# Statistics of the first layer on VectorE for six batches in place of three, under a rewritten order of steps, in a two-layer graph kernel

## The chip, the cores and the metric

The kernel runs on one core of a Trainium2 chip. The metric is the device time of one execution in microseconds (us). The kernel before was run three times: 2301.16, 2302.13 and 2302.11 us, median 2302.11.

The core's engines run side by side, each through its own queue of instructions in order: PE (TensorE) multiplies matrices, DVE (VectorE), ACT (ScalarE) and POOL (GpSimd) work on tiles, SP (SyncE) issues most of the DMA transfers, ACT and POOL issue some. An instruction starts when those ahead of it on its engine are through and the semaphores that it waits for have been raised.

## The reference, cut to what matters

`x` is 32 batches of 512 channels by 1024 nodes, in float32. Two residual layers follow one another:

```python
# layer 0: attention over nodes, mixed by adj
h = relu(layernorm(x))                       # over the 1024 nodes
q, k = wq . h, wk . h                        # one number per node
s = leaky_relu(q[n] + k[m], 0.01)
att = softmax(s, over n)
x = x + relu(adj @ (h @ att^T) + bm)
# layer 1: two graph products
h = relu(layernorm(x))
x = x + ((support * kernel) applied to h) + bias     # support and kernel are both adj
```

The layer norm divides by the root of the variance plus 1e-5. Both layers need the mean and the variance of every row of 1024 elements: 4 tiles of 128 channels per batch and layer.

## The kernel before, in words

**The work of a batch.** The score of a pair is a sum of two numbers under a leaky ReLU. So the softmax is not taken over a 1024 by 1024 matrix: nodes are sorted by q, and for each m the sums over the nodes above and below a threshold come out of running totals. A batch goes through these steps, each a function in the kernel:

- `load` (L309, SP) brings four tiles of 128x1024. `stats` (L315 on) takes mean and variance of one tile. `norm` and `slopes` turn them into a scale and a shift, `relu` (L366, ACT) applies them.
- `scores` (L375, PE) gives q and k, which go through DRAM and come back as a row on all partitions (`row`). `rank` (L417 to L426, DVE) counts, for 128 nodes, how many q are smaller; `lower` (L433, ACT) counts against k. `value` (L474, PE) is adj times h for 128 nodes, `spread` (L481, ACT) copies it from PSUM, and `scatter` (L487, POOL) writes it by rank to a DRAM table `td`.
- `fetch` (L503, SP) reads the sorted rows into the tiles `vs`. `weights` (L512 and after, ACT) takes the exponentials, `later`, `totals` (L535, L536, PE) and `stationary` (L546, POOL) prepare the running sums.
- `scan` (L562, and L559 for the middle one, PE) makes the running sums of 128 rows with a triangular matrix; nine scans (0 to 8) per batch, each from both ends. The last row of one scan must be in the next one's input: `sums` (L574 copies the result out of PSUM on ACT) carries that row over. For batches 5 to 27 (`LO = 5`, `HI = 4`) it is carried by two DMAs of 2 KB on SP (L576, L577, `vs<-t` in the profile); for the others by two copies on ACT (L572, L573). Two more DMAs (L580, L581) put the sums into `td`.
- `gather` (L586, POOL) fetches the rows for each m, into one buffer `G` that all batches share. `excess`, `divide`, `weigh` (L611, ACT) and `combine` (L615, DVE) make the softmax's result, `turn` (L622 PE, L626 DVE) transposes it, adds it to x and leaves row sums for layer 1.
- Layer 1: `means`, `stats` (the Square alone, L337), `norm`, `slopes`, `relu`, then the graph product: `seed`, `mix`, `propagate` (L657, PE) and `finish` (L670, L674, DVE) in a form with seven half-size products; the last four batches (`PLAIN = 4`) use plain products (`plain`, L689). `store` (L701, SP) writes the result.

**Statistics of layer 0.** `stats` has two ways. For `s.b < DIRECT` it runs on DVE: two `bn_stats` of 128x512 (L324) and one `bn_aggr` (L325) per tile. For other batches it runs on ACT: one `Identity` (L334) and one `Square` (L337) of 128x1024 per tile, each with an accumulated sum.

**The order.** All steps of all batches, 5935 of them, are issued in one fixed order that stands in the string `ORDER`: two characters in base 36 per step, which name the kind of step and how many steps of that kind to skip ahead. `tc.manual_schedule()` keeps that order on every engine's queue. So the steps of four to six batches are interleaved: while batch 14 scans, batch 12 is in its second layer, 13 is gathered, 16 is ranked and 17 loaded. In the steady part the order repeats every 187 steps, one batch. Bounded buffers add waits: 8 PSUM banks, 16 tiles for x and h (`xp`), 5 fetched tiles (`vsp`), 2 tiles for sums (`tp`) and one `G`.

The switch and the scan's carry, as they stand before:

```python
if layer == 0 and s.b < DIRECT:          # DIRECT = 3
    ...
    nc.vector.bn_stats(st[:, i, :], s.x[c][:, ts(i, HALF)])
    nc.vector.bn_aggr(s.mv[:, c, :], st.rearrange("p i s -> p (i s)"))
    return
...
nc.scalar.copy(t[:, 0:C], p)             # sums, of scan i
if i < NB - 1 and LO <= s.b < B - HI:
    nc.sync.dma_start(s.vs[ha - 1][0:1, 0:C], t[0:1, 0:C])
    nc.sync.dma_start(s.vs[hb + 1][HP : HP + 1, 0:C], t[HP : HP + 1, 0:C])
```

Of the kernel before, what the change touches and what calls it, by code (L numbers as in the profile page):

```python
# [26 lines left out]
DIRECT = 3  # L27
# [6 lines left out]
0a0405002u2y2w302u2y01022w30342y362w352u3730342w322u332y3538303b3639033a2i102j2k180u0d090v12080n0l  # L34
0q0g0x130s370p0f320o0z150b0m0i0t0y33170r0h380c3b110e1639343a1i0w190j061d0k10352w302y1j142z2i361e2l
0u1f371g2m321b2j2k180v1a33121h380x1c133b0z0l0n150q2l0y0g0s2n170p0f39110o0i160m0h0w190t3a070e0r101i
1d2o312u0j2w142u1b0u2p0k1a1c2m2q2i3u3v1j1k1e2k180v1t1f2j1g121l131h0x1u1m150z0n0l3w1v2l1n0g0q0y1w0f
0s1o170i0p111x0h0o1p0e160m0w2n1y1i1a0j191b341q2y0k2x1d2v1z1j1e351r1f141g0t1h0r362m1c3732332o382p2q
3u3b1k20391s3a1t2i3v1l2k21101u2j1m18220u1v3w25291n120l0n270v1w262l280g0q1o23130x1x240f0s0i1p0p0z15
0h2n1y0o0e1q170m0y1i1d1z0j1b340k1a1r11161j1e352r1f362s0w1g191h0t141c0r2e2m375e2d5d322c332a5c385b2o  # L40
59553b2p56202q3u5a1k391s3a1t2i3v1l2k21102f2g5g1u5i5h5f0u2j2b18582h575k5j1m123m3q1v3w3n3t3r3o0n1n3p
0q3s0v221w250s0l290p1o270x2t130g1x26283e2l231p0f0z3h242n1y0i3g1q150h3f0y1z0e3c0o3d1r1i1d17113j0j3i
1b0m4t1a4u3l0w0k3k4w16344v1j1e41302x2r3x422s1f352y4g1g434n3y3z444f191h4036454m2z464i2o0t2p474x3u20
4y4p49500r4z4k1s141c4h37482m513v212q1k324r2e4b332d2c5e385c4a2u4j1t5b594d4o3b5a1l5d392w4l524c3a531u
2i4q1m314e2a2v3w1v55562k104s2j2f2g542b5i2h585k1n18570u5j1w5h5g0l0n1o0q5f3m3n1x3o3p3q3t0s1p123r0p3s
2n0v221y250g291q13272t0x0f3e261z282l231r0i3h240z153g0h3f0y0e173c0o3d0m1i1a113j0j3i1b340k1d0w4t3l1j
1g3k4u4w351f41304v312z2x424g3x2r202s434n3y1s4f3z4044161e2136454m464i191h0t472o4x4y0r4z49502e4p372p
484h3u5e3v2d5d4b324r2c332a4a5c2f384j554d3b2y4o5652395b4c593a5a2q2g2u1k4q2b2i5i2w582v574e5h5g1t5f2k
104s2h4k2j5k545j514l1l2m1853141c3m3n1u3o3p3q3t1m0n3r3s1v3w0u220q250s290l1n12270p0v2t261w0g283e2l23
1o0x240f1x3h0i1p133g0z0h2n1y0e3f1q153c1i1d0o0y3d1z0j1b3j1a1r0k3i110m4t3l4u1j1g3k4w0w342r4v3x2s3y43  # L50
2z3z313530444f171f454m2y1640201e414i2o1s4g191h2p42363u2q3v46144n0t1c2e1k4x0r4p474y1t4z3750485e5d4k
2149324r2d332c1l4h2a5c38514b553b565b4a394j2u593a4d5a2w4o1u2f2m4c2g2b2h2i2v4q2x58525k4e5i572k104s5j
542j5h5g5f1m4l18533m3n1v3w3o3p3q3t3r3s0n0u220q250s291n0l12270p0v261w2t0g3e283f232l0x240f3g131o3h0i
0z1x3c0o3d150h3j0y3i0e0m4t3l4u1p3k1i1d114w342n4v1b0j1y1a3x2r410k3y35444g1j1g3z434m172s401f1645194f
361e424i1h2e464n0t5e2d5d0w0r4x4y2c4p2a502f4z2g554830141c5c312b2z562o1q2y582h4r492p1z5k3u375b2q1k4h
4a5i5932574b332u4o385j524c3b4j5a395h1r2x4q3a4d5g2w5f202m1t4e2i4s4l102v54532j1s181l213v2k3m1u3n3o3p
3q3t3r3s0u220n250q290s1m0l2747120p3w2t0g1v260v3e284k3h0f23513g0x242l0i3f1n133c0z0o0h1w0m3d150e3j0y
3i1i1d340j1b1o4t113l1a4u0k1x3k354w414v1j1g422r4g3x2s3y1p171f4n3z43162n1y1e4044194f1h36454m2h0t465k
5j2b4i0r0w4x4y2g4p2f502a4z2c55482d305831141c5c2e2z49562o2y4r5b1q4h2p4a375i3u59574b2u4o1z5e322q1k4j
4c335a52385h4d3b2w4q2x5d395g1r2v5f3a4e4l2m201t2i4s1054532j1s181l213v2k3m1u3n3o3p3q3t3r3s0u220n250q  # L60
291m0l0s270v121v3w2t0p0g263e282l0x230f3h24131n3g0i47151w3f0h0z3c0o3d0m4k0e511o3j0y1x1i1d3i0j341b11
4t1a4u3l0k3k354w1p4v411j1g2n1y2r3x422s171f3y4g3z444n40161e1943364m1h454f2e0t5e465d2d4i0r5c0w4x2c4y
2a4p2f502g4z2b485530141c31562o2z5b2h1q2v4r492p581z3u5i372q1k4h4a5k5932574b332x4o385j524c3b4j5a395h
1r2y4q3a4d5g2u5f202m1t4e2i4s4l102w54532j1s181l213v2k3m1u3n3o3p3q3t3r3s0u220n250q290s1m0l2747120p3w
2t0g1v260v3e284k3h0f23513g0x242l0i3f1n133c0z0o0h1w0m3d150e3j0y3i1i1d340j1b1o4t113l1a4u0k1x3k354w41
4v1j1g422r4g3x2s3y1p171f4n3z44162n1y1e4043194m1h36454f2e0t465e5d2d4i0r0w4x4y2c4p2a502f4z2g55482b30
5c31141c562h2z495b2o2v4r581q4h2p4a375i3u5k592q2x1k4o1z4b5732335j384c4j523b5a5h4d2y394q2u5g3a1r5f2w
4l4e2m53201t2i4s10541s181l2j213v2k3m1u3n3o3p3q3t3r3s0u220n250q290s1m0l2747120p3w2t0g1v260v3e284k3h
0f23513g0x242l0i3f1n133c0z0o0h1w0m3d150e3j0y3i1i1d340j1b1o4t113l1a4u0k1x3k354w414v1j1g422r4g3x2s3y
1p171f4n3z44162n1y1e4043194m1h36454f2e0t465e5d2d4i0r0w4x4y2c4p2a502f4z2g55482b305c31141c562h2z495b  # L70
2o2v4r581q4h2p4a375i3u5k592q2x1k4o1z4b5732335j384c4j523b5a5h4d2y394q2u5g3a1r5f2w4l4e2m53201t2i4s10
541s181l2j213v2k3m1u3n3o3p3q3t3r3s0u220n250q290s1m0l2747120p3w2t0g1v260v3e284k3h0f23513g0x242l0i3f
1n133c0z0o0h1w0m3d150e3j0y3i1i1d340j1b1o4t113l1a4u0k1x3k354w414v1j1g422r4g3x2s3y1p171f4n3z44162n1y
1e4043194m1h36454f2e0t465e5d2d4i0r0w4x4y2c4p2a502f4z2g55482b305c31141c562h2z495b2o2v4r581q4h2p4a37
5i3u5k592q2x1k4o1z4b5732335j384c4j523b5a5h4d2y394q2u5g3a1r5f2w4l4e2m53201t2i4s10541s181l2j213v2k3m
1u3n3o3p3q3t3r3s0u220n250q290s1m0l2747120p3w2t0g1v260v3e284k3h0f23513g0x242l0i3f1n133c0z0o0h1w0m3d
150e3j0y3i1i1d340j1b1o4t113l1a4u0k1x3k354w414v1j1g422r4g3x2s3y1p171f4n3z44162n1y1e4043194m1h36454f
2e0t465e5d2d4i0r0w4x4y2c4p2a502f4z2g55482b305c31141c562h2z495b2o2v4r581q4h2p4a375i3u5k592q2x1k4o1z
4b5732335j384c4j523b5a5h4d2y394q2u5g3a1r5f2w4l4e2m53201t2i4s10541s181l2j213v2k3m1u3n3o3p3q3t3r3s0u
220n250q290s1m0l2747120p3w2t0g1v260v3e284k3h0f23513g0x242l0i3f1n133c0z0o0h1w0m3d150e3j0y3i1i1d340j  # L80
1b1o4t113l1a4u0k1x3k354w414v1j1g422r4g3x2s3y1p171f4n3z44162n1y1e4043194m1h36454f2e0t465e5d2d4i0r0w
4x4y2c4p2a502f4z2g55482b305c31141c562h2z495b2o2v4r581q4h2p4a375i3u5k592q2x1k4o1z4b5732335j384c4j52
3b5a5h4d2y394q2u5g3a1r5f2w4l4e2m53201t2i4s10541s181l2j213v2k3m1u3n3o3p3q3t3r3s0u220n250q290s1m0l27
47120p3w2t0g1v260v3e284k3h0f23513g0x242l0i3f1n133c0z0o0h1w0m3d150e3j0y3i1i1d340j1b1o4t113l1a4u0k1x
3k354w414v1j1g422r4g3x2s3y1p171f4n3z44162n1y1e4043194m1h36454f2e0t465e5d2d4i0r0w4x4y2c4p2a502f4z2g
55482b305c31141c562h2z495b2o2v4r581q4h2p4a375i3u5k592q2x1k4o1z4b5732335j384c4j523b5a5h4d2y394q2u5g
3a1r5f2w4l4e2m53201t2i4s10541s181l2j213v2k3m1u3n3o3p3q3t3r3s0u220n250q290s1m0l2747120p3w2t0g1v260v
3e284k3h0f23513g0x242l0i3f1n133c0z0o0h1w0m3d150e3j0y3i1i1d340j1b1o4t113l1a4u0k1x3k354w414v1j1g422r
4g3x2s3y1p171f4n3z44162n1y1e4043194m1h36454f2e0t465e5d2d4i0r0w4x4y2c4p2a502f4z2g55482b305c31141c56
2h2z495b2o2v4r581q4h2p4a375i3u5k592q2x1k4o1z4b5732335j384c4j523b5a5h4d2y394q2u5g3a1r5f2w4l4e2m5320  # L90
1t2i4s10541s181l2j213v2k3m1u3n3o3p3q3t3r3s0u220n250q290s1m0l2747120p3w2t0g1v260v3e284k3h0f23513g0x
242l0i3f1n133c0z0o0h1w0m3d150e3j0y3i1i1d340j1b1o4t113l1a4u0k1x3k354w414v1j1g422r4g3x2s3y1p171f4n3z
44162n1y1e4043194m1h36454f2e0t465e5d2d4i0r0w4x4y2c4p2a502f4z2g55482b305c31141c562h2z495b2o2v4r581q
4h2p4a375i3u5k592q2x1k4o1z4b5732335j384c4j523b5a5h4d2y394q2u5g3a1r5f2w4l4e2m53201t2i4s10541s181l2j
213v2k3m1u3n3o3p3q3t3r3s0u220n250q290s1m0l2747120p3w2t0g1v260v3e284k3h0f23513g0x242l0i3f1n133c0z0o
0h1w0m3d150e3j0y3i1i1d340j1b1o4t113l1a4u0k1x3k354w414v1j1g422r4g3x2s3y1p171f4n3z44162n1y1e4043194m
1h36454f2e0t465e5d2d4i0r0w4x4y2c4p2a502f4z2g55482b305c31141c562h2z495b2o2v4r581q4h2p4a375i3u5k592q
2x1k4o1z4b5732335j384c4j523b5a5h4d2y394q2u5g3a1r5f2w4l4e2m53201t2i4s10541s181l2j213v2k3m1u3n3o3p3q
3t3r3s0u220n250q290s1m0l2747120p3w2t0g1v260v3e284k3h0f23513g0x242l0i3f1n133c0z0o0h1w0m3d150e3j0y3i
1i1d340j1b1o4t113l1a4u0k1x3k354w414v1j1g422r4g3x2s3y1p171f4n3z44162n1y1e4043194m1h36454f2e0t465e5d  # L100
2d4i0r0w4x4y2c4p2a502f4z2g55482b305c31141c562h2z495b2o2v4r581q4h2p4a375i3u5k592q2x1k4o1z4b5732335j
384c4j523b5a5h4d2y394q2u5g3a1r5f2w4l4e2m53201t2i4s10541s181l2j213v2k3m1u3n3o3p3q3t3r3s0u220n250q29
0s1m0l2747120p3w2t0g1v260v3e284k3h0f23513g0x242l0i3f1n133c0z0o0h1w0m3d150e3j0y3i1i1d340j1b1o4t113l
# [690 lines left out]
```

## Time and profile before

| | before |
|---|---|
| median of three runs | 2302.11 us |
| profiled execution | 2301.56 us |
| its span | 2299.8 us |
| PE busy | 2215.1 us (96%) |
| DVE busy | 1719.3 us (75%) |
| ACT busy | 1730.8 us (75%) |
| POOL busy | 716.9 us (31%) |
| mean granted clock of PE | 0.988 |
| DMA | 657.77 MB, 286 GB/s on the mean |

All times in the profile are of one execution on the chip and count from the start of its span. The span is a little shorter than the execution's time; the 1.8 us around it are the same kind of overhead in every run. A table by stretch gives each engine's busy time between two moments. A wait is written as the engine and line that waited, an arrow, and what it waited for, with the total, the count and the longest. The chain of work that ended last is followed back from the last instruction: at each step to what released it, or to the instruction before it on its engine; it is listed as start, length, engine, tile and line. `x8` behind an instruction is a count.

### The profile page before, as it was taken

The page shows a single profiled execution, that of the slowest core. Times are in us where ns is not written, and L with a number is a line of the kernel's source. Part 1 is how long each engine was busy: PE and PEld are TensorE (multiplying, and loading weights), DVE is VectorE, ACT ScalarE, POOL GpSimd, SP SyncE. Part 2 cuts the span into 40 slices and gives each one's busy share as a digit, 9 for nine tenths or more (in the row PEclk, how much of TensorE's full clock was granted, in tenths as well). Part 3 has the DMA queues.
Part 4 walks back from the last instruction along what each step waited for, and adds up shares of the span by engine and source line. Part 5 has one row for each costly group of instructions (what it writes and reads, how often), then busy time and mean ns, then how long its engine had stood idle before and what let it go on. Part 6 is the DMA issues. An engine that isn't in the chain of part 4 may idle for free.

```text
span 2299.8 us, 28792 instructions
## 1 busy us (share of the span) xinstructions
PE 2215.1 (96%) x7344; PEld 946.6 (41%) x7344; DVE 1719.3 (75%) x4840; ACT 1730.8 (75%) x3317; POOL 716.9 (31%) x979
## 2 busy tenths in 40 slices
PE   6978999999999999999999999999999999999897
PEld 3423443444444444444444444344444444443343
DVE  6746777878778778877877877877877787777453
ACT  4699889776778777777877777877777887787752
POOL 2343223333323333233333222333332333224210
PEclk9989999999999999999999999999999999999999
DMA  6676878888889888888888878888888888877961
GB/s 225 234 282 232 282 293 309 313 298 295 274 291 324 296 311 291 286 291 317 308 310 298 298 267 310 317 301 305 294 275 290 323 300 305 311 246 277 356 243 64
DMA packets 217717, 657.77 MB, mean 286 GB/s; under 512 B 39376, under 2 KB 39504, under 8 KB 217552
## 3 DMA queue, kind: packets, MB, share of 16 engines
q1 hardware_dynamic: 153760, 362.16, 46.7%
q0 software_dynamic: 57344, 276.86, 31.3%
q10 hardware_dynamic: 6448, 16.92, 2.8%
q8 instruction: 59, 0.97, 0.2%
q14 instruction: 106, 0.87, 0.1%
HBM read 438.05 MB, written 217.01 MB: 285 GB/s over the span
## 4 chain that ended last, share of the span: by engine, by line
PE 77%; DMA 8%; ACT 6%; DVE 5%; issue 2%; POOL 1%; SPq 0%; ACTq 0%; POOLq 0%; DVEq 0%
PE pv L474 34%; PE pg L657 26%; PE sc L562 9%; PE tr L622 3%; DMA td<-t 3%; PE pq L375 2%; DVE g L615 2%; DMA g<-td,idg 2%; PE pp L689 1%; PE sc L559 1%; ACT junk L433 1%; DVE y L626 1%; ACT junk L337 1%; DMA td<-v,idx 1%; DMA vs<-t 1%
## 5 line engine op out<-in xcount | busy, mean ns | idle before, releaser
L474 PE MATMUL pv<-wmT,x 128*128 128x512 f32 x2048 | 917.5, 596 | 0.0
L474 PEld LDWEIGHTS pv<-wmT,x 128*128 128x128 f32 x2048 | 380.5, 190 | 489.1 <-issue 452.1
L487 POOL DMA_INDIRECT td<-v,idx x256 | 270.7, 1057 | 659.5 <-issue 283.5
L657 PE MATMUL pg<-h,wsq 128*128 128x512 f32 x896 | 412.4, 602 | 2.5 <-DVE y L674 2.0
L615 DVE SCALAR_TENSOR_TENSOR g<-g,cf 128x512 f32<-128x512 f32 x512 | 375.2, 764 | 17.2 <-ACT g L611 14.0
L586 POOL DMA_INDIRECT g<-td,idg x256 | 244.8, 956 | 299.2 <-DVE y L626 95.2
L433 ACT ACTIVATE junk<-qrow,qk 128x1024 uint8<-128x1024 f32 x256 | 292.8, 1144 | 30.3 <-DMA qrow<-qd 19.9
L562 PE MATMUL sc<-vs,sm 128*64 128x512 f32 x1024 | 284.0, 621 | 7.8 <-ACT vs L572 5.8
L657 PEld LDWEIGHTS pg<-h,wsq 128*128 128x128 f32 x896 | 163.3, 190 | 243.3 <-issue 180.9
L574 ACT COPY t<-sc 128x512 f32<-128x512 f32 x288 | 167.6, 582 | 99.2 <-PE sc L562 41.6
L481 ACT COPY v<-pv 128x512 f32<-128x512 f32 x256 | 147.4, 578 | 124.3 <-PE pv L474 77.4
L546 POOL TENSOR_TENSOR sm<-mask_a,wc 128x192 f32<-128x192 f32 x96 | 63.2, 658 | 521.4 <-PE sc L562 455.9
L657 PE MATMUL pg<-mx,wmix 128*128 128x512 f32 x448 | 209.4, 599 | 0.0
L366 ACT ACTIVATE x<-x,nmr,rstd 128x1024 f32<-128x1024 f32 x128 | 149.3, 1230 | 78.2 <-DVE nmr L359 78.2
L670 DVE SCALAR_TENSOR_TENSOR y<-pg,bm_sb,y 128x512 f32<-128x512 f32 x224 | 166.4, 745 | 45.9 <-PE pg L657 45.5
L422 DVE TENSOR_SCALAR_CACHE_REDUCE junk<-qrow,qk,cnt 128x128 uint8<-128x128 f32 (+6 forms) x224 | 180.4, 805 | 8.2
L626 DVE SCALAR_TENSOR_TENSOR y<-tr,nbm,y 128x512 f32<-128x512 f32 x256 | 174.7, 746 | 15.3 <-PE tr L622 12.4
L417 DVE TENSOR_SCALAR_CACHE_REDUCE junk<-qrow,qk 128x896 uint8<-128x896 f32 (+6 forms) x224 | 165.7, 740 | 18.6 <-DMA qrow<-qd 16.7
L674 DVE TENSOR_TENSOR y<-pg,y 128x512 f32<-128x512 f32 x168 | 115.1, 685 | 81.6 <-PE pg L657 81.1
L611 ACT ACTIVATE g<-g,cf 128x512 f32<-128x512 f32 x256 | 168.6, 709 | 3.4 <-DVE cf L605 1.7
L337 ACT ACTIVATE junk<-y,nm 128x1024 uint8<-128x1024 f32 x128 | 146.7, 1146 | 31.4 <-DVE nm L345 29.6
L366 ACT ACTIVATE h<-y,nmr,rstd 128x1024 f32<-128x1024 f32 x128 | 154.0, 1235 | 2.6 <-DVE nmr L359 2.6
(135 smaller groups left out, 2496.4 us busy)
## 6 DMA issues: line engine op xcount, KB each, us to landing
vs<-td SPq DMA_DIRECT2D x96, 792.0 KB
td<-t SPq DMA_DIRECT2D x576, 132.0 KB
x<-in_x_dram SPq DMA_DIRECT2D x128, 512.0 KB
y<-in_x_dram SPq DMA_DIRECT2D x128, 512.0 KB
out_dram<-y SPq DMA_DIRECT2D x128, 512.0 KB
qrow<-qd ACTq DMA_DIRECT2D x32, 512.0 KB
vs<-t SPq DMA_DIRECT2D x368, 2.0 KB
td<-v,idx POOLq DMA_INDIRECT x256, 6.3
```

Of the source, the lines that this page charges most:

```text
L337: nc.scalar.activation(junk, s.x[c], AF.Square, bias=s.nm[:, c : c + 1], scale=1.0 / ROOT, accum_out=s.var[:, c : c + 1],)
L366: nc.scalar.activation(h, s.x[c], AF.Relu, bias=s.nmr[:, c : c + 1], scale=s.rstd[:, c : c + 1])
L422: nc.vector.tensor_scalar(junk[:, j * P :], s.qrow[:, j * P :], qc, first, ALU.is_lt, ALU.add, accum_out=s.cnt[:, 1, j : j + 1],)
L433: nc.scalar.activation(junk, s.qrow, AF.Sign, bias=s.qk[:, 1, j : j + 1], accum_out=s.sgn[:, j : j + 1])
L474: nc.tensor.matmul(pv, s.h[c][:, ts(j, P)], wmT[:, c, :], start=(c == 0), stop=(c == NC - 1))
L487: i = nc.gpsimd.indirect_dma_start(tds[s.b % TABLES][:, :], bass.IndirectOffsetOnAxis(ap=s.idx[j // 4][:, j % 4 : j % 4 + 1], axis=0), v[: ...
L562: nc.tensor.matmul(p[ts(k, HP), :], m[:, k, :], s.vs[h][:, 0:C], start=True, stop=True)
L586: nc.gpsimd.indirect_dma_start(s.g[:, j, :], None, tds[s.b % TABLES].rearrange("(s k) w -> s k w", k=3), bass.IndirectOffsetOnAxis(ap=s.id ...
L611: nc.scalar.mul(r, r, s.cf[:, 0, j : j + 1])
L615: nc.vector.scalar_tensor_tensor(r, s.g[:, j, k * W : k * W + C], s.cf[:, k, j : j + 1], r, ALU.mult, ALU.add)
L626: nc.vector.scalar_tensor_tensor(xh, pt, nbm[:, o : o + 1], xh, ALU.max, ALU.add, accum_out=s.ys[:, i, o : o + 1])
L657: nc.tensor.matmul(s.pg[key], forms[m][:, r, ts(u, P)], data, start=(m == 2 and r == 0), stop=(r == 1), skip_group_check=True,)
```

## The change

`DIRECT` goes from 3 to 6: the first-layer statistics of batches 3, 4 and 5 are taken on DVE rather than on ACT. And `ORDER` is replaced as a whole: the same 5935 steps, nearly all of them at other places in the sequence. No other line changes.

```diff
-DIRECT = 3
+DIRECT = 6
 ...
 ORDER = """
-0a0405002u2y2w302u2y01022w30342y362w352u3730342w322u332y3538303b3639033a2i102j2k180u0d090v12080n0l
 ...
```

In the instruction streams, ACT has 24 activations fewer, DVE has 24 `bn_stats` and 12 `bn_aggr` more; PE has the same 4224 matmuls, SP the same 1442 transfers. In the steady part, between scan 1 and scan 5 of batch 14, PE has this order of steps (batch:step, transposes of batch 12 between scans 1 and 2 left out):

```
before  14:scan1  16:value0  14:scan2  11:propagate6  16:value1  16:value3
        14:scan3  16:value5  16:value4  14:scan4  16:value7  12:propagate0  12:propagate1  14:scan5
after   14:scan1  16:value2  14:scan2  16:value6  16:value0
        14:scan3  16:value1  16:value5  14:scan4  16:value7  12:propagate0  14:scan5
```

Between scan 5 and scan 6 the new order has correspondingly more. At the start, before the sort of batch 0, the new order has two statistics tiles fewer and two `pads` steps more on DVE; at the end, the turns of batch 28 stand earlier among PE's steps.

## The prediction

> **What bounds the kernel now.** I read the page's first part, the table of busy time by stretch, the waits of PE, and the chain of work in the stretches where PE is not full.
>
> ```profile
> PE 2215.1 (96%) x7344; PEld 946.6 (41%) x7344; DVE 1719.3 (75%) x4840; ACT 1730.8 (75%) x3317; POOL 716.9 (31%) x979
> ```
> ```profile
> 100.00:150.00 50.00, 37.72 (x128) 13.60 (x128) 21.91 (x83) 44.75 (x91) 14.17 (x25) 0.86 0.61 204
> 150.00:200.00 50.00, 40.12 (x135) 15.65 (x134) 29.25 (x101) 45.62 (x92) 21.26 (x30) 0.90 0.74 271
> ...
> 400.00:2000.00 1600.00, 1591.95 (x5365) 682.90 (x5364) 1262.70 (x3552) 1219.12 (x2343) 520.90 (x701) 1.00 0.86 299
> ...
> 2100.00:2200.00 100.00, 87.26 (x263) 35.83 (x262) 56.75 (x125) 68.49 (x134) 26.27 (x29) 0.95 0.84 313
> 2200.00:2300.00 100.00, 80.75 (x225) 38.21 (x223) 42.20 (x92) 33.60 (x53) 7.51 (x8) 0.95 0.33 129
> ```
> The columns are length, busy PE, PEld, DVE, ACT, POOL, granted clock, DMA share, GB/s. PE bounds the middle: 8 us idle in 1600. Its 85 idle us lie at the ends: 18.7 in the first 50 us, 22 between 100 and 200, 32 after 2100. From 100 to 200 ACT is 90% busy and PE idles.
>
> ```profile
> PE pd L535 <- ACT w L512: 20.6, 2, 11.4
> ...
> PE sc L559 <- DMA vs<-t: 1.3, 2, 1.2
> PE sc L562 <- DMA vs<-t: 1.0, 3, 0.6
> ```
> ```profile
> 136.59 0.38 PE L535 MATMUL pd<-w,mask_a 128*64 128x9 f32 x2 [11.36 <-ACT w L512]
> ...
> 137.51 4.56 PE L562 MATMUL sc<-vs,sm 128*64 128x512 f32 x8
> ```
> Two waits, 11.36 us at 136.59 (batch 1) and 9.21 at 189.39 (batch 2), are for the attention weights on ACT. Eight scan matmuls behind the first take 4.56 us, at 1021 they take 1.87; the granted clock of these two stretches is 0.86 and 0.90. The carry rows (vs<-t) hold PE for only 2.3 us in all. The next two fences are the chain at batch 7 and the chain in a steady batch.
> ```profile
> 562.29 0.59 ACT t L574
> ...
> 563.48 5.13 DMA vs<-t
> ...
> 568.75 1.10 PE sc L559 x2
> ```
> ```profile
> 1030.21 1.01 PE sc L562 x4
> 1031.22 1.91 PE pg L657 x4
> 1033.13 6.87 PE pv L474 x16
> 1040.00 1.01 PE sc L562 x4
> ...
> 1048.93 3.43 PE pv L474 x8
> 1052.36 3.43 PE pg L657 x8
> 1055.80 1.01 PE sc L562 x4
> ```
> A scan needs the last row of the one before it: copy on ACT, issue on SP, 2 KB DMAs. At batch 7 scan 3 ended at 562.26 and scan 4 started at 568.75: 6.5 us, with 5.2 us of PE work to cover it (PE waited the rest). At 1030 scans 2 and 3 stand 8.8 us of PE work apart, and it is covered.
>
> **The change, part by part.** The sum goes against the profiled execution, 2301.56 us (span 2299.8 and 1.8 around it), 0.55 below the median of 2302.11.
>
> *Statistics.* Twelve tiles (batches 3 to 5) leave ACT: an Identity (L334, 1.05 us and its 0.19 read) and a Square (L337, 1.15 and 0.19), 2.34 us from tile to tile, 28.1 us in all. DVE gets twelve times two bn_stats (a pair takes 1.28) and a bn_aggr, 1.44 us from tile to tile, 17.3 us. PE's work is the same. ACT's four tiles of batch 3 (120.6 to 134.9) stand directly ahead of batch 1's weights, and batch 4's four ahead of batch 2's.
>
> *Start, on ACT.* I add the durations along each engine's own order up to batch 1's totals: PE 106.6 us in both orders, ACT 87.2 before and 78.0 after. So the weights come about 9.2 us sooner against the same PE work, and of the 11.36 us some 2.2 are left. Up to batch 2's totals ACT falls from 138.2 to 128.7 and PE's work ahead of them grows from 148.5 to 162.8: 24 us of new room against a wait of 9.21, which goes. Behind the waits the slow scans and scores (4.56 and 3.98 for 1.87, 2.43 for 1.86) are worth 5.4 us, small waits 0.8. Together 26.8 us can come back, less the 2.2.
>
> *Start, on DVE.* What is late next is DVE. Up to batch 1's totals its queue grows from 91.8 to 100.4 us, up to batch 2's from 121.4 to 147.1. It idled 9.0 us at 22.6 (bias), 4.5 at 67, 5.0 at 96, 9.9 at 120 and 8.0 before 146, which is most of the cover. But in the new order two statistics tiles fewer go ahead of the bias wait (which ends at 31.58 all the same) and five pads in place of three behind it, so batch 0's ranks start at about 40 in place of 35.4, and all behind them on DVE and POOL (scatters, then the fetch that weights wait for) comes 2 to 4 us later. Batch 0's totals may then wait 0 to 4 us, batch 3's relu holds PE for 2 to 3. I take 4.5 for these beside the 2.2. Start: 26.8 - 2.2 - 4.5, a gain of 20. Bounds: 26.8 with none of the new waits; 2.8 if 17.3 of DVE's new work lay on the path besides these. Nearer to the first, as DVE's idle time is real.
>
> *Steady state.* Each batch takes 187 steps in both orders; what differs here is the order alone. Carry rows go by DMA for batches 5 to 27. Between scan 2 and scan 3 the order before has a propagate and two values on PE (1.91 + 6.87 = 8.8 us); the new one has two values only, 6.9. Between scan 4 and 5 it has a value and one propagate (3.43 + 1.72 = 5.2) for a value and two (6.9). Before scan 1, 6 and 8 there is 1.8 to 3.5 more; at scan 4 the same 6.8; at scan 7 1.8 less, where 3.2 were spare. From the packets of the two rows I read, over batches 8 to 22, a median from issue to landing of 6.2 us behind scan 2, 5.2 behind scan 3, 3.8 behind scan 4 and 2.0 behind scan 1: the eight gathers (128 rows each, from 1029 on) and then the scatters fill the DMA engines in just that time (share 0.96 to 1.03 from 1031 to 1050). With the copy (0.59 and up to 0.7 until ACT is free), the issues (0.6 for the second) and about 0.5 from landing to the matmul, scan 3 is due 7.4 to 8.4 us after scan 2 whatever PE does. Against 6.9 that is a wait of 0.5 to 1.5 us, 0.95 in the middle, in some 20 batches (7 to 24, 26, 27): 19 us. Behind scan 4 the path is 4.0 to 6.2 against 5.2 in 16 batches: 0.2 each, 3 us. The 2.3 us that rows cost now go for the most part. Loss: 20 us. Bounds: 9 (0.4 per batch, if ACT is free at once) and 40 (1.5 and 0.6 per batch). The row at batch 7 (6.5 us with ACT free at once and 5.13 of DMA) is the nearest, and it speaks for the middle.
>
> *Queues passed.* SP's loads and reloads, moved too, wait for tiles that values release; in both orders they stand between the rows of scan 5 and those of scan 7, with over 14 us of PE work ahead of scan 6. Nothing, as long as no value comes later than scan 6. POOL's gathers stay behind the turns. Last turns to the next layer's first propagate: 25.5 us of PE work before, 23.6 after, over an ACT chain of about 22 to 24: nothing to 0.3 us per batch, within the bounds above.
>
> *End.* After 2050 the batches hang on one gather buffer: turns of a batch, gather (15 us to landing), combines, turns, 45.8 to 46.6 us per batch. But from batch 27's last turn (2056.4) to 28's (2115.8) it takes 59.4, as PE's order has other work ahead. The new order puts 28's turns 14.4 us earlier in PE's order. Bounds of the gain: nothing, and 59.4 - 46.6 = 12.8. DVE then has mixes and finishes of batch 27 among the combines of 28, which takes part of it: I take 6.
>
> Sum: 2301.6 - 20 - 6 + 20 = 2295.6, about 2296.
>
> **The rivals.** Rows that wait longer (slower): every 0.1 us more per batch costs 2. At 1.5 us at scan 2 and 0.6 at scan 4 the loss is 40 and the time 2316; from 31 us of loss on (1.5 us per batch over some 20 batches) the change is slower than before by 0.2%. For it: PE has 1.9 and 1.7 us less cover at the two places where rows are slowest. Against it: rows wait at two to five scans now.
>
> DVE late at the start (slower or the same): if 10 to 17 of its new 17.3 us fall on the path, the start gains 10 to 3 and the time is 2306 to 2313. For it: batch 0's ranks start 4 to 5 us later. Against it: 36 us of idle time up to 146.
>
> Rows that don't wait (faster): if gathers stand otherwise against the scans and rows land as behind scan 1 (2.0 us, 4 to 5 in all), both new distances are enough, the loss is none, and the time is 2301.6 - 26 - 2 = 2274. The Trainium skill (DMA: Bandwidth & Descriptors, Anatomy of one DMA) gives a transfer about 2.0 us of fixed cost plus its bytes at 436 GB/s, stated for the gpsimd path; by that alone a row of 2 KB would land in 2 us and this rival would hold. The trace has 5.13 us for one, so I give it little.
>
> **How the numbers follow.** As forecast: 0.52, own range 2288 to 2304, of which 0.34 lie below 2297.5 and 0.18 within 0.2% (4.6 us, about what a measurement of this kernel can tell from no change). Rows that wait longer: 0.23, slower for 0.21. DVE late: 0.15, slower for 0.13. Rows that don't wait: 0.10, faster. Faster 0.44, same 0.22, slower 0.34. The range 2279 to 2317 leaves out 0.1 below and some 0.08 above.
>
> **What would show it.** In the profile after: the wait of L535 on L512 falls from 20.6 us to below 5; PE between 100 and 200 rises from 77.8 busy us to over 92 and the granted clock to 0.95 or more; the waits of L562 and L559 on vs<-t rise from 2.3 us to 10 to 40, about one for each batch, in front of scan 3; PE's idle time from 400 to 2000 rises from 8 to 20 to 35; after 2050 the turns of batch 28 end 46 to 54 us behind those of 27. I would be wrong if DVE's ranks or the scatter show as PE's wait before 150, or if PE's idle time in the middle stays near 8.

## The result and the profile after

The kernel after takes 2299.68 us on the median of 20 runs, the kernel before 2302.14 on the median of 20; the ratio is 0.9976, with a 95% interval from 0.9968 to 0.9985. So the change makes the kernel 0.24% faster, some 5.5 us by the ratio; the two medians lie 2.5 us apart. The forecast was 2296 us, 6 us less than before. The profiled execution took 2299.28 us with a span of 2297.6, 2.2 us less than the span before; the sums below go against that.

The page's first part and the table by stretch of the kernel after (columns as before: length, busy PE, PEld, DVE, ACT, POOL, granted clock, DMA share, GB/s):

```profile
PE 2225.3 (97%) x7344; PEld 954.0 (42%) x7344; DVE 1735.6 (76%) x4876; ACT 1703.1 (74%) x3269; POOL 704.9 (31%) x979
```
```profile
100.00:150.00 50.00, 46.63 (x186) 17.48 (x183) 35.97 (x121) 43.74 (x90) 22.89 (x36) 1.00 0.76 253
150.00:200.00 50.00, 49.77 (x185) 21.11 (x184) 44.09 (x134) 43.26 (x88) 19.45 (x27) 1.00 0.70 257
...
400.00:2000.00 1600.00, 1582.20 (x5251) 680.36 (x5252) 1237.86 (x3475) 1202.77 (x2313) 496.21 (x691) 1.00 0.83 294
...
2100.00:2200.00 100.00, 96.21 (x311) 40.98 (x310) 66.73 (x151) 72.62 (x145) 28.69 (x32) 1.00 0.86 319
2200.00:2300.00 100.00, 77.87 (x193) 35.70 (x191) 36.89 (x83) 33.61 (x53) 7.55 (x8) 0.88 0.32 126
```

From 100 to 200 PE is busy for 96.4 us, before for 77.8, and its granted clock there is 1.00. From 2100 to 2200 it has 96.2 for 87.3. In between, from 400 to 2000, it has lost 9.8: idle for 17.8 us in place of 8.0. The waits of PE over the whole run:

```profile
PE sc L562 <- DMA vs<-t: 11.8, 12, 2.3
...
PE pq L375 <- ACT x L366: 10.7, 1, 10.7
...
PE pd L535 <- ACT w L512: 1.2, 1, 1.2
```

The wait for weights has fallen from 20.6 us to 1.2, the wait for carry rows risen from 2.3 to 11.8. More of it is hidden, as the next lines show: PE's instructions around scans 2 and 3 of batch 14 in the kernel after.

```profile
1027.42 1.08 PE L562 MATMUL sc<-vs,sm 128*64 128x512 f32 x4
1028.43 7.13 PE L474 MATMUL pv<-wmT,x 128*128 128x512 f32 x16
1035.68 1.40 PE L562 MATMUL sc<-vs,sm 128*64 128x512 f32 x4
1037.01 7.13 PE L474 MATMUL pv<-wmT,x 128*128 128x512 f32 x16
```

Scan 2 takes 1.08 us for its four matmuls, scan 3 1.40. A scan has two halves, and each needs a row of its own; the first half starts when its row is there, and the second then waits inside the scan. The table of waits doesn't count that, and the table by stretch counts it as busy. Counted as the scan's length over 1.08 (1.02 for the middle scan) plus the idle time ahead of it, and added over batches 5 to 27:

| wait at | scan 0 | scan 1 | scan 2 | scan 3 | scan 4 | scan 5 | scan 8 |
|---|---|---|---|---|---|---|---|
| before, us | 0.9 | 1.4 | 0.1 | 1.3 | 2.3 | 0.0 | 1.5 |
| after, us | 8.2 | -0.5 | 8.6 | 21.4 | 1.3 | 0.0 | 1.3 |

Where the time went can be followed batch by batch: the start of scan 2 in the kernel after less that in the kernel before, less the difference of PE's work ahead of it in the two orders (mean durations by step). What is left is the lead, in us, minus being ahead:

| scan 2 of batch | 1 | 2 | 5 | 8 | 14 | 22 | 27 | 30 | 31 | end of the span |
|---|---|---|---|---|---|---|---|---|---|---|
| lead | -9.6 | -21.3 | -19.3 | -11.5 | -4.5 | -1.3 | +6.5 | +7.1 | -4.8 | -2.2 |

So in this profile the start gains 19 to 21 us, the middle costs 26 (from -19.3 to +6.5), and the end gains 9. The start's figure is the highest of those that follow: in seven more profiles with the same steps up to scan 2 of batch 3 the lead there is 15.7 to 19.6 us.

### The profile page after: what moved, and what is told of

It reads as the page before. It is cut to its first block, busy times and chain, and to the rows that moved or that the text cites. A ratio compares the mean times of both kernels' runs of the same rounds, so it can differ in the third digit from the quotient of the medians.

```text
span 2297.6 us, 28803 instructions
## 1 busy us (share of the span) xinstructions
PE 2225.3 (97%) x7344; PEld 954.0 (42%) x7344; DVE 1735.6 (76%) x4876; ACT 1703.1 (74%) x3269; POOL 704.9 (31%) x979
## 5 line engine op out<-in xcount | busy, mean ns | idle before, releaser
L474 PE MATMUL pv<-wmT,x 128*128 128x512 f32 x2048 | 919.2, 598 | 0.7 <-ACT x L366 0.6
L474 PEld LDWEIGHTS pv<-wmT,x 128*128 128x128 f32 x2048 | 378.5, 190 | 496.5 <-issue 440.2
L487 POOL DMA_INDIRECT td<-v,idx x256 | 261.4, 1021 | 525.6 <-DVE junk L417 218.5
L657 PE MATMUL pg<-h,wsq 128*128 128x512 f32 x896 | 416.5, 599 | 5.2 <-DVE y L674 3.7
L615 DVE SCALAR_TENSOR_TENSOR g<-g,cf 128x512 f32<-128x512 f32 x512 | 365.9, 750 | 9.1 <-ACT g L611 6.5
L562 PE MATMUL sc<-vs,sm 128*64 128x512 f32 x1024 | 298.2, 615 | 18.7 <-DMA vs<-t 11.8
L657 PEld LDWEIGHTS pg<-h,wsq 128*128 128x128 f32 x896 | 165.0, 190 | 236.2 <-issue 183.5
L670 DVE SCALAR_TENSOR_TENSOR y<-pg,bm_sb,y 128x512 f32<-128x512 f32 x224 | 166.8, 746 | 95.6 <-PE pg L657 95.5
L657 PE MATMUL pg<-mx,wmix 128*128 128x512 f32 x448 | 213.4, 600 | 1.3 <-ACT pg L648 1.3
L626 DVE SCALAR_TENSOR_TENSOR y<-tr,nbm,y 128x512 f32<-128x512 f32 x256 | 174.9, 746 | 31.7 <-PE tr L622 21.4
L422 DVE TENSOR_SCALAR_CACHE_REDUCE junk<-qrow,qk,cnt 128x640 uint8<-128x640 f32 (+6 forms) x224 | 180.4, 805 | 8.2
L417 DVE TENSOR_SCALAR_CACHE_REDUCE junk<-qrow,qk 128x384 uint8<-128x384 f32 (+6 forms) x224 | 165.8, 740 | 3.6 <-DMA qrow<-qd 1.7
L562 PEld LDWEIGHTS sc<-vs,sm 128*64 128x64 f32 x1024 | 62.3, 135 | 200.7 <-issue 128.7
```

The costliest lines, as they stand in the source:

```text
L422: nc.vector.tensor_scalar(junk[:, j * P :], s.qrow[:, j * P :], qc, first, ALU.is_lt, ALU.add, accum_out=s.cnt[:, 1, j : j + 1],)
L474: nc.tensor.matmul(pv, s.h[c][:, ts(j, P)], wmT[:, c, :], start=(c == 0), stop=(c == NC - 1))
L487: i = nc.gpsimd.indirect_dma_start(tds[s.b % TABLES][:, :], bass.IndirectOffsetOnAxis(ap=s.idx[j // 4][:, j % 4 : j % 4 + 1], axis=0), v[: ...
L562: nc.tensor.matmul(p[ts(k, HP), :], m[:, k, :], s.vs[h][:, 0:C], start=True, stop=True)
L615: nc.vector.scalar_tensor_tensor(r, s.g[:, j, k * W : k * W + C], s.cf[:, k, j : j + 1], r, ALU.mult, ALU.add)
L626: nc.vector.scalar_tensor_tensor(xh, pt, nbm[:, o : o + 1], xh, ALU.max, ALU.add, accum_out=s.ys[:, i, o : o + 1])
```

## The experiments

### Start, middle and end by themselves

The two orders hold the same steps, so one can be followed up to some step and the other from there on, the steps already done left out. The orders are nearest to each other at step 936 (one step differs), just ahead of scan 2 of batch 5, and near step 4857, around scan 1 of batch 26 (four differ). Four kernels were put together at these places:

```diff
 start_only:  DIRECT = 6;  steps 0-935 new order,  936- old order
 mid_only:    DIRECT = 3;  0-935 old,  936-4858 new,  then old
 end_only:    DIRECT = 3;  old up to scan 1 of batch 26,  then new
 start_end:   DIRECT = 6;  0-935 new,  old up to scan 1 of batch 26,  then new
```

> The new order and DIRECT = 6 up to the 936th step (just before scan 2 of batch 5), the order before from there on. Theory (three separate parts; against equal PE work the new kernel was 19 to 21 us ahead at batch 5): a gain of 19, about 2283 us, ratio near 0.992; the waits of PE for carry rows stay at the 2 to 3 us of before. Rival (what the start gains is given back because something else, a DMA pace for one, sets the steady part): 2299 to 2302.

> DIRECT = 3 and the order before, but steps 936 to 4858 (batch 5's scan 2 to batch 26's scan 1) in the new order. Theory: the loss is in the steady order itself, some 21 us at scan 3, 8 at scan 0, less at other places, minus what the order before waits: 22 to 26 us more, about 2326 us, ratio near 1.011. Rival (the steady part only takes back the head start): no change, 2302.

> DIRECT = 3 and the order before up to batch 26's scan 1, the new order from there. Theory: the earlier turns of batch 28 gain 9 to 12 us, less 4 for scan 2 of batches 26 and 27 waiting for its rows in the new order: 2294 to 2297, ratio 0.997. Rival (the gather buffer sets the end whatever the order): 2302.

> DIRECT = 6, new order up to the 936th step, the order before up to batch 26's scan 1, the new order from there. Theory (the parts add): 2302 - 19 - 7 = 2276 us, ratio near 0.989, faster than both kernels. Rival: as the kernel after, 2299.

| | median, us | ratio to before | 95% interval |
|---|---|---|---|
| start_only | 2293.19 | 0.9953 | 0.9935 to 0.9971 |
| mid_only | 2331.41 | 1.0123 | 1.0103 to 1.0144 |
| end_only | 2300.47 | 0.9985 | 0.9974 to 0.9997 |
| start_end | 2287.97 | 0.9938 | 0.9919 to 0.9957 |

The signs are those of the theory: the middle alone makes the kernel slower, without any head start that it could take back; the start and the end alone make it faster, and together they add. The rival, that the middle only takes back the head start, falls: from batch 5 to batch 26 the lead of mid_only falls by 22.5 us (from -1.4 to +21.1), and that of the kernel after by 23.4 (from -19.3 to +4.1). In start_only's profile the lead is -9.3 us at batch 7 and -9.7 at batch 26: from batch 7 on, nothing is given back under the old order.

The sizes were off: 2283 us were expected of start_only, 2326 of mid_only, 2294 to 2297 of end_only, 2276 of start_end. The seams, the places where one order is left for the other, are a large part of the reason, and they taught more than the sizes. In start_only the seam leaves 3.4 us of PE work between scans 4 and 5 of batch 5, and scan 5 waited 4.1 us; in mid_only scan 4 of batch 5 waited 4.5; in end_only 3.4 us stand in front of scan 3 of batch 26, and it waited 6.1. At the same two seams start_end waited 2.8 and 4.5. They show the rule at another size: where the work between two scans is shorter than the way of the row, the scan waits for about the difference (6.9 us of work in front of scan 3 cost 0.9, 3.4 us in front of a scan cost 3 to 6). The seams don't explain all: from batch 3 to 7 the lead of start_only falls by 6.4 us, of which the wait at scan 5 is 4.1; the rest I have not placed.

### Seams moved

```diff
-start: change over at step 936      +start: change over at step 823
-end:   at scan 1 of batch 26        +end:   behind scan 6 of batch 27 (step 5223)
```

> As start_only, but changed over at step 823 in place of 936. At 936 the seam leaves only 3.4 us of PE work between scan 4 and scan 5 of batch 5; at 823 batch 5 has the distances of the order before (6.8). Theory (a scan waits when the PE work in front of it is shorter than the way of its row): the 4.1 us at that seam go, 2293 - 4 = 2289 us, ratio against before 0.9935. Rival (the start's gain is given back in the steady part): 2293 or more.

> As end_only, but changed over at step 5223 (behind scan 6 of batch 27), so that batches 25 to 27 keep the distances of the order before and no seam leaves 3.4 us in front of scan 3 of batch 26 (it waited 6.1 us there). Theory (the end's gain is 12 us, from the earlier turns of batch 28, and scans 2 and 3 of batches 26 and 27 took most of it): 2303 - 10 to 12 = 2292 us, ratio 0.995. Rival (the end is set by the gather buffer): 2300.

> DIRECT = 6; the new order up to step 823, the order before up to step 5223, the new order from there. Theory: start and end add, 2303 - 14 - 11 = 2278 us, ratio near 0.989, the fastest of all. Rival: as start_end with its seams, 2288, ratio 0.994.

| | median, us | ratio to before | 95% interval |
|---|---|---|---|
| start_clean | 2296.39 | 0.9958 | 0.9944 to 0.9971 |
| end_clean | 2295.24 | 0.9960 | 0.9946 to 0.9973 |
| start_end_clean | 2284.56 | 0.9909 | 0.9894 to 0.9925 |

The new end with batches 25 to 27 left in the old order is worth 0.40% for 0.15% with them in the new one. The 2292 us expected of it were missed by 3. The new start is no better with its other seam: 2289 us were expected of start_clean, and it took the time that the rival names. The wait at scan 5 is gone, but PE now waits for something else. Up to 420 us it waits 7.2 us for the copies that open the second layer's product, where the kernel after and start_only have 2.4 and 2.5:

```profile
PE pg L657 <- ACT pg L648: 7.2, 4, 4.7
```

start_end_clean has the same wait there (7.3 us), so it belongs to this order of steps. Whether it is a cost of the seam or a part of the head start that the old order can't keep, no run shows.

start_end_clean takes the new start and the new end and keeps the old middle. It has the lowest median of all, 0.9% under the kernel before and, by the two ratios, 0.7% under the kernel after; expected were 2278 us, and its interval overlaps that of start_end. Its profile by stretch:

```profile
100.00:150.00 50.00, 46.00 (x183) 17.03 (x182) 35.21 (x119) 41.02 (x84) 22.39 (x36) 1.00 0.74 239
150.00:200.00 50.00, 49.48 (x182) 20.87 (x180) 44.34 (x137) 43.41 (x91) 18.66 (x24) 1.00 0.73 272
400.00:2000.00 1600.00, 1589.63 (x5334) 681.35 (x5334) 1256.88 (x3541) 1222.07 (x2350) 520.95 (x701) 1.00 0.85 299
```

The start is nearly that of the kernel after (95.5 us busy from 100 to 200, for 96.4) and the middle nearly that of the kernel before (10.4 us idle).

### The statistics apart from the order

```diff
 old_order_d6:   ORDER of before,  -DIRECT = 3  +DIRECT = 6
 new_order_d3:   ORDER of after,   -DIRECT = 6  +DIRECT = 3
```

> DIRECT = 6 under the order of before, all steps where they were. Theory (ACT's queue ahead of batch 1's and 2's weights is what PE waits for): four tiles fewer ahead of the first wait, 9.4 us, eight fewer ahead of the second; waits of L535 on L512 fall from 20.6 to about 2, DVE takes 5.8 and 11.5 us more in its idle time, the steady part stays: 2302 - 18 to 20 = 2283 us, ratio 0.992. Rival (DVE's queue becomes what the weights wait for, so that the order has to be rewritten for it): half of that, 2292 or more.

> DIRECT = 3 under the new order. The new order has all eight statistics tiles of batches 3 and 4 and two of batch 5 ahead of batch 1's weights; on ACT these are 10 times 2.34 = 23.4 us more. Theory: ACT's work ahead of batch 1's totals grows from 78 to 101 us, 14 more than in the kernel before, where the wait was 11.4: about 25 us of wait there and 2300 + 22 to 26 = 2324 us, ratio near 1.009. Rival (the new order alone makes the start): 2300.

old_order_d6 took 2304.59 us, ratio 0.9994 (0.9981 to 1.0006): the same as before. The theory as I had written it falls; the rival had the right engine, DVE, but expected half of the gain, and there is none. ACT has 9.4 us less work ahead of batch 1's weights, and they come hardly sooner. The wait is still there, as PE's waits up to 250 us show; behind it, the chain that ends in the weights:

```profile
PE pd L535 <- ACT w L512: 18.9, 2, 10.4
```
```profile
130.66 0.23 DVE arg L467
130.89 1.21 DVE st L324 x2
...
132.12 0.22 DVE mv L325
...
132.37 0.31 ACT std L349
...
132.98 0.20 ACT w L512
```

On ACT's queue the norm of batch 3 (L349) stands directly ahead of batch 1's weights. It needs batch 3's statistics. Those are on DVE now, at the place in the order where ACT had them, behind ranks and a from_rows (L467) that itself waited for ACT. ACT idles 4.32 us in front of L349. Before, the four tiles kept ACT busy to 134.9; now it waits for DVE to 132.4, a gain of 2.6 us. At batch 2 it is the same again: ACT idles 3.0 us in front of L349, and PE's wait there is 10.4 us, for 9.21 before. So the 20 us of the start need both: the statistics on DVE, and an order that issues them long before the norm. In the new order all tiles of batches 3 and 4 stand ahead of batch 1's weights, in the old one the four of batch 3 alone.

new_order_d3 took 2322.06 us, ratio 1.0082 (1.0063 to 1.0100), near the 2324 of the theory. At batch 2 its lead is -1.2 us for -21.3 in the kernel after. ACT's queue is the bound there, in the table by stretch:

```profile
100.00:150.00 50.00, 39.73 (x125) 14.43 (x124) 22.90 (x83) 47.93 (x97) 11.25 (x20) 0.90 0.53 182
```

ACT is busy for 47.93 of 50 us and PE for 39.73. The place of the wait was not the one expected: L535 waits 4.2 us up to 250, and scans wait besides, 4.5 us, for their carry copies (L572, L573), which queue behind the statistics; the rest I have not placed. So neither part of the change, the statistics or the order as a whole, makes the kernel faster without the other.

### The two waits of the steady part

```diff
 new_scan3_cover (after, batches 8 to 24):
-11:propagate13  11:finish13  11:store3  ...  14:scan1  ...  14:scan2  16:value6  16:value0  14:scan3
+14:scan1  ...  14:scan2  11:propagate13  16:value6  11:finish13  16:value0  11:store3  14:scan3
 new_later_first (after, batches 9 to 22):
-14:weights0  12:reload1  11:finish2  14:later0
+14:weights0  14:later0  12:reload1  11:finish2
```

> The kernel after with one step moved for batches 8 to 24: the last propagate of batch b-3 (with its finish and store) goes from ahead of scan 1 to just behind scan 2 of batch b, so that 8.7 in place of 6.9 us of PE work stand between scan 2 and scan 3, as in the order before. Theory (scan 3 waits 0.9 us per batch for rows that land 6 us after their issue): that wait goes in 17 batches, 2300 - 15 = 2285 us, ratio against before near 0.992; scan 1 stays without a wait. Rival (the wait only moves, to scan 1 with 1.8 us less cover or to scan 4): 2298 to 2300.

> The kernel after with one step moved for batches 9 to 22: DVE's two adds of later (L523) go ahead of a finish (L670) that stands before them. Theory (scan 0 takes 1.54 in place of 1.08 us because its second mask on POOL is late, and that because later stands behind the finish): 0.46 us in 14 batches, 2300 - 6 = 2294 us, ratio against before 0.995. Rival (POOL's mask is late for another reason, or PE waits elsewhere for the finish): 2300.

new_scan3_cover did at scan 3 what was expected: from batch 8 to 24 scan 3 waits nowhere, where it waited 0.9 us a batch. But the kernel took 2305.39 us, ratio 1.0005 (0.9995 to 1.0015), which is slower than the kernel after. From batch 8 to 22 it has gained 6.3 us on the kernel after (958.3 us for 964.7), less than the 13 taken away at scan 3. Scan 1, which has 1.8 us less work in front of it, waited 1.8 us at batch 11 and 2.6 at batch 17 (and 4.2 at batch 8, just ahead of that stretch), and scan 4 waits 4.5 us in all where it waited 1.3. That is the rival, in part. How much of scan 1's wait comes from its shorter cover is open: under the order of before scan 1 waits 1.6 us over batches 8 to 24 in the profile of the kernel before and 7.7 in that of end_clean. The 6.3 us gained were lost beforehand: at batch 8 the lead is -4.8 us for -11.5, and at batch 22 the two kernels are level. The wait at scan 1 of batch 8 is 4.2 us; and at batch 3 already the lead is -17 us, 4 less than that of the kernel after, though the two have the same order up to there. What it lost behind batch 22 I can't name.

new_later_first took 2297.23 us, ratio 0.9961 (0.9946 to 0.9975); the kernel after has 0.9976, and the intervals overlap. In the profile the effect is plain. Scan 0 in the kernel after, with POOL's masks and DVE's queue beside it:

```profile
1001.31 1.54 PE L562 MATMUL sc<-vs,sm 128*64 128x512 f32 x4
```
```profile
1000.16 1.09 POOL L546 TENSOR_TENSOR sm<-mask_a,wc 128x192 f32<-128x192 f32 x1 [6.18 <-PE pg L657]
1001.21 0.51 POOL L546 TENSOR_TENSOR sm<-mask_b,wc 128x192 f32<-128x192 f32 x1
```
```profile
998.33 0.75 DVE L670 SCALAR_TENSOR_TENSOR y<-pg,bm_sb,y 128x512 f32<-128x512 f32 x1
999.18 0.69 DVE L674 TENSOR_TENSOR y<-pg,y 128x512 f32<-128x512 f32 x1
999.79 0.36 DVE L523 TENSOR_SCALAR wc<-w,ident 128x9 f32<-128x9 f32 x2
```

The second mask ends at 1001.72, and the scan's second half can't start earlier. It is late because later's two adds (L523) stand on DVE behind two finishes; their input, the weights, was there at 997.1. (The bracket behind the first mask names PE; the run decides, as only DVE's order differs in it.) With later put first, scan 0 takes 1.11 us in place of 1.54 in all 14 batches, 6 us together. The stretch from batch 8 to 22 shrinks from 964.7 to 958.3 us, which by itself would say little: two profiles of one order differ by as much there.

### The gathers behind scan 3

```diff
 new_gathers_late (after, batches 8 to 24), on POOL's queue:
-13:gather0 ... gather1  14:scan2  13:gather7 ... gather2  14:scan3
+14:scan2  14:scan3  13:gather0 ... gather2
```

> The kernel after, with the eight gathers of batch b-1 moved from around scan 2 to behind scan 3 of batch b on POOL's queue, for batches 8 to 24. Theory (the rows behind scan 2 land late because the gathers fill the DMA engines then): they land in 2 to 3 us, scan 3 takes 1.08 us and waits for nothing, and scans 4 and 5, whose rows then travel beside the gathers with 6.9 and 5.2 us of PE work, wait 0.5 to 2 us in their place; the turns wait for gathers that come 9 us later. Rival (the rows take 6 us by themselves): scan 3 takes 1.7 us as before.

It took 2324.16 us in one run. PE's waits from 400 to 2000 have turned to the rows altogether:

```profile
PE sc L562 <- DMA vs<-t: 28.0, 22, 2.2
```

Scan 3's wait goes (0 in most batches, 5.0 us in all for 21.4), and scan 5, which never waited, waits 1.3 to 3.8 us in nearly all of batches 8 to 24, 30.6 in all. That much is as the theory says: the wait goes where the gathers go. But the rows behind scan 2 did not land in 2 to 3 us. Their median from issue to landing is 5.0 for 6.0. POOL doesn't wait for PE's scans, so the gathers moved by a few us only: at batch 14 the two rows were issued at 1035.47 and 1036.05, and the first gather at 1035.48. The rows then met the gathers' front.

What the run does show is in the rows behind scan 4. In the kernel after they travel when the gathers are through, and land in 2.6 us; here the gathers run beside them, and they land in 5.0 (medians over batches 8 to 22). Behind scan 2 the first packet of a row now starts 1.2 us after the issue in place of 3.8. And in the kernel after, between the issue and the landing of the rows behind scan 2, packets of the gathers fill the 16 DMA engines for 5.8 of the 6.0 us on the mean, and SP's own packets for 0.1. By queue, from 1029 to 1044 (q0 is POOL's, with gathers and scatters, q1 is SP's; packets, MB, share of the time of 16 engines):

```profile
q0 software_dynamic: 1010, 5.69, 92.3%
q1 hardware_dynamic: 351, 0.40, 7.4%
```

So a row that travels beside the gathers comes 2 to 4 us later than one that doesn't, and the wait goes to the scan behind it. A kernel in which no row meets them was not run.

## Why the prediction was right, point by point

**Start, a gain of 20 us.** Measured: 19.3 to 21.3 in the profile of the kernel after, from 15.7 on in others with the same steps. The large terms held: L535's wait was forecast to keep 2.2 us and keeps 1.2; both slow stretches behind the waits are gone, the granted clock there is 1.00. The 4.5 us for new waits were right in size only, by luck: batch 0's totals wait for nothing, batch 3's relu holds PE for 0.6 us in place of 2 to 3, and the first scores (L375, batch 0), which were not named, wait 10.7 us in place of 8.7. DVE did not become the bound, though it does 17.3 us more. But the reason that the prediction gave, less work in ACT's queue ahead of the weights, was half of the reason. The sums over the new order's queue were right because that order also has the statistics early; the same edit under the old order gains nothing, since ACT's queue then holds an instruction that waits for DVE.

**Steady part, a loss of 20.** Measured: 26. The largest term, 0.95 us at scan 3 in some 20 batches, 19 us, was right in place and nearly in size: 16.9 us in the batches that it names, 0.85 a batch, and 4.5 more at batch 6, which it left out. Two terms of the step failed. Scan 4's rows were given 3 us and cost none; they landed in 2.6 us in place of 3.8, as they now travel at another place against the gathers and scatters. And two places were missed: scan 0, 0.46 us a batch, 8 in all, where DVE's order delays a mask (nothing of it shows among the waits of before); and scan 2 of batches 5, 6 and 25 to 27, 8.6 in all. On the other side PE's time at turns and propagates is 7.8 us less; of that, 2.2 us are waits that went, and the rest I have not placed. For PE's time from scan 2 of batch 8 to scan 2 of batch 22, by the line whose start it runs from:

| line | before, us | after, us |
|---|---|---|
| scans L562 | 113.4 | 126.8 |
| values L474 | 392.5 | 396.5 |
| propagates L657 | 350.3 | 346.1 |
| turns L622 | 52.5 | 48.9 |
| all | 954.4 | 964.7 |

That is 0.73 us a batch net, where scans 0 and 3 alone cost 1.4. The forecast's total came out near by luck, in two ways: here, since the missed terms and the missed gains are of one size, and in the whole, since 6 us too little for the loss stand against 3 too little for the end.

**End, a gain of 6.** Measured: 9. From batch 27's last turn to 28's it takes 46.7 us (2062.4 to 2109.1) for 59.4, near the lower end of the 46 to 54 that were named. The turns that end the two batches, before and after:

```profile
2053.60 2.78 PE L622 MATMUL tr<-ident,g 128*128 128x128 f32 x24
...
2114.90 1.04 PE L622 MATMUL tr<-ident,g 128*128 128x128 f32 x8
```
```profile
2061.71 0.65 PE L622 MATMUL tr<-ident,g 128*128 128x128 f32 x4
...
2104.76 4.30 PE L622 MATMUL tr<-ident,g 128*128 128x128 f32 x32
```

**Rows that don't wait**, the rival that the Trainium skill's price of about 2.0 us a transfer (DMA: Bandwidth & Descriptors, Anatomy of one DMA) would give, did not come. The price itself agrees with the trace where the engines have room: behind scan 1 and scan 6 rows land in 2.3 and 2.0 us in the kernel after. Behind scan 2 they take 6.0, at a DMA share of 0.97 to 1.02 from 1029 to 1044.

**What would show it.** Three of the five signs came as named, one in part, one not. The waits for rows came to 11.8 us, within 10 to 40, but 12 times rather than once for each batch, and some in front of scan 2. PE's idle time from 400 to 2000 is 17.8 us, for 20 to 35 forecast. In both a part of the waits lies inside scans and is not counted as idle.

## What to carry to other kernels

Moving work off a full engine gained nothing here until the work was also issued earlier on the other engine: an instruction of the full engine that needs the moved result holds all behind it. In an order written out by hand, check for each carried value how much work stands between producer and consumer, and compare it with the way's length at that moment, not with its shortest; and judge a rewritten order by stretches, since here a start worth 0.4% and an end worth 0.4% were all but used up by a steady part with 0.7 us more per batch. The table of waits can miss a wait that falls between the halves of one group of matmuls: look for a group that has grown longer.

## What was not expected of the hardware

The same steps in the same order take different times from run to run. Up to batch 5 the kernel after, start_only, start_end, new_scan3_cover and new_later_first are the same, and their leads at batch 3 are -21.3, -15.7, -17.5, -17.0 and -18.6 us. The largest difference is in end_clean. It has the order of before up to batch 27, and its profile is 2 us behind the kernel before at batch 8, 10 at batch 22 and 15 at batch 27; the profiled execution took 2306.87 us, the median of its six runs is 2295.24. So a single profile fixes a part of this kernel to some 5 us, and at times only to 15, and the 2.2 us between the two profiled spans say less than the ratio over 20 runs. What this document rests on came more than once: the waits at scans 0 and 3 in the profiles of the kernel after and of mid_only (8.1 and 21.4 us, 8.5 and 19.8), the signs of start, middle and end in the medians of several runs.
